# Softmax attention: turning the maxima on VectorE and gathering them by way of DRAM, in place of transposes on TensorE

## The chip, the core and the metric

The kernel runs on one core of a Trainium2 chip. A core has TensorE (PE in the profile, with its weight loads as PEld), VectorE (DVE), ScalarE (ACT), GpSimd (POOL), and SyncE (SP), which here only issues DMAs. The metric is the device time of one execution in microseconds. Before the change it is 2184.47 us, the median of three runs from 2184.06 to 2188.18.

## The reference

The input x has 2 sequences of 2048 tokens with 256 features each. The program is a chain of four residual blocks, each on a layer-normalized x: softmax attention (16 query heads in 4 groups over 4 key heads, head size 16), a feed-forward block of three rotation cycles, a linear causal attention, and the feed-forward block again. The change lies in the first of them:

```
q = x @ Wq + bq;  k = x @ Wk + bk;  v = x @ Wv + bv
scores = einsum('bghnd,bhsd->bghns', q, k)
attn   = softmax(scores / 4, axis=-1)
out    = einsum('bghns,bhsd->bghnd', attn, v)
return out.transpose(...).reshape(B, N, 256) @ Wo + bo
```

Everything is float32. The softmax subtracts each query's largest score before it takes the exponential.

## The kernel before

The attention is worked in 32 **units**. A unit is one block of 512 queries (8 blocks over the two sequences) in one of the 4 groups, with all 4 key heads r. Each unit is passed over twice.

The **first pass**, the generator `largest()`, finds the maxima. It has 64 steps per unit: for each of 4 key blocks of 512, 4 blocks of 128 queries (qi) and 4 heads (r), PE multiplies 128 queries by 512 keys into a PSUM tile `s` (L378, three banks, tag "s"), and VectorE reduces it to its maximum in a column of `mx` (L382). Behind the 64th step VectorE reduces `mx` to the negative maxima `nm` (L390) and splits each into two parts, a rounded one (L392) and the rest (L393). Both lie in `mt`, with queries on the partitions.

The **second pass** needs these numbers as rows, with the 512 queries along the free dimension. `turn_maxima` (L395) does that: four PE transposes into one PSUM bank `pm` (L398), a ScalarE copy of its 8 rows to `mr` (L402), and four small DMAs (L405) into `mrows`, two sets of two tiles that alternate from unit to unit. The row tiles are `a_m` in the profile.

In the second pass, for each unit and each of 16 key blocks of 128 (kb), PE computes transposed scores `p`, keys by queries, for four heads (L633). It adds the negative maxima by a second matmul into the same bank, `pick` times the rows of `mrows` (L637, the shift), ScalarE takes the exponential (L641), and PE multiplies the result by the values one iteration later (`weigh`, L620, eight matmuls in the trace). The four banks of `p`, with tag "p", are also where `pm` and other small results are put.

One iteration over kb therefore calls for four steps of the first pass (`next(ahead)`) and one of the second. The first pass runs 80 steps ahead. Its 64 steps for unit u+1 are done as kb 12 of unit u begins. Then `turn_maxima` is put in the list `later`; it is taken up at the beginning of kb 13, run behind that iteration's exponentials and ahead of its `weigh`. The rows are first read by the shifts in kb 0 of unit u+1. For unit 0 all of it falls into the prologue, where it runs at n == 67.

Other work around it: `finish` (L449) takes the sum of a unit in the kb loop of the next, over DMAs to DRAM and back (`ds`, `rs`, `dr`, `sums`, L465 to L475), and for every fourth unit multiplies by the output weights (L487) in four successive iterations, kb 10 to 13. `norm` (L414) prepares the next stage's input with PE transposes (L425). `project(u + 2)` stores a unit's queries to DRAM (L244) and loads them in the layout that both passes use (L249, `qP`, three buffers). Near the beginning of the loop the weights of the later stages are loaded (L686).

The order of instructions on each engine is written out by hand for the prologue (`in_order`, the SP queue among them) and again for the later stages. In the attention loop a scheduler puts the instructions of each engine in order by the program's order and by when it reckons them ready, so a transfer that is ready can go ahead of one that is not.

Of the kernel before, what the change touches and what calls it, by code (L numbers as in the profile page):

```python
# [9 lines left out]
F32 = mybir.dt.float32  # L10
F32R = mybir.dt.float32r
AF = mybir.ActivationFunctionType
ALU = mybir.AluOpType
AX = mybir.AxisListType
PSUM = bass.MemoryType.PSUM

P = 128
B, N, D = 2, 2048, 256
T = B * N
BLK = 512  # L20
# [4 lines left out]
KV = 4  # L25
# [42 lines left out]
def tile_hybrid(ctx: ExitStack, tc: tile.TileContext, x: bass.AP, consts: bass.AP, wa_d: bass.AP, wf_d: bass.AP, wb_d: bass.AP, out: bass.AP):  # L68
    nc = tc.nc
# [11 lines left out]
    dram = ctx.enter_context(tc.tile_pool(name="a_dram", bufs=2, space=bass.MemoryType.DRAM))  # L81
# [3 lines left out]
    def const(name):  # L85
        return small[:, _CONST[name][0] : _CONST[name][1]]
# [4 lines left out]
    ident, mean_w, ones = const("ident"), const("mean"), const("ones")  # L91
# [44 lines left out]
    def in_order(first, which=(engines.PE, engines.DVE, engines.Activation, engines.Pool)):  # L136

        last = {}
        for ins in nc.cur_bb.bb.instructions[first:]:
            if ins.engine in which:  # L140
                if ins.engine in last:
                    tc.add_manual_dep(
                        ins, last[ins.engine].name,
                        mybir.DependencyInfo(mybir.DependencyClass.NoSync, mybir.DependencyReason.DATA),
                        reason="order of the program",
                    )
                last[ins.engine] = ins
# [5 lines left out]
    def attention_a():  # L153
        with ExitStack() as st:
# [8 lines left out]
            mrows = [[hold.tile([P, BLK], F32R, name=f"a_m{i}_{p}") for p in range(2)] for i in range(2)]  # L163
# [10 lines left out]
            sb = st.enter_context(tc.tile_pool(name="a_sb", bufs=2))  # L174
            pss = st.enter_context(tc.tile_pool(name="a_s", bufs=3, space=PSUM))
            psp = st.enter_context(tc.tile_pool(name="a_p", bufs=4, space=PSUM))
# [182 lines left out]
                queries[u] = qP  # L359
                return lambda: fetch(qP, d)  # L360

            later = []

            def largest():


                for u, (j, g) in enumerate(units):
                    k0 = (j // BPB) * N
                    qP = queries[u]
                    mx = sb.tile([P, 4, KV, 4], F32, tag="mx", name=f"mx{u}")  # L370
                    first = u == 0

                    def step(kb, qi, r):

                        pool, tag = (psp, "p") if first and (4 * qi + r) % 5 > 2 else (pss, "s")
                        s = pool.tile([P, BLK], F32, tag=tag, name=f"s{u}_{kb}_{qi}_{r}")
                        row = slice(64 * (r % 2), 64 * (r % 2) + 64)
                        mm(  # L378
                            s, qP[r // 2][row, qi * P : (qi + 1) * P],
                            kP[r // 2][row, k0 + kb * BLK : k0 + (kb + 1) * BLK], start=True, stop=True,  # L380
                        )
                        nc.vector.tensor_reduce(mx[:, qi, r : r + 1, kb], s, AX.X, ALU.max)  # L382

                    for kb in range(4):
                        for qi in range(4):
                            for r in (0, 1, 3, 2):
                                step(kb, qi, r)
                                yield
                    nm = sb.tile([P, 4, KV], F32, tag="nm", name=f"nm{u}")
                    nc.vector.tensor_reduce(nm, mx, AX.X, ALU.max, negate=True)  # L390
                    mt = sb.tile([P, 4, KV, 2], F32, tag="mt", name=f"mt{u}")
                    nc.vector.tensor_copy(mt[:, :, :, 0].bitcast(F32R), nm)  # L392
                    nc.vector.tensor_tensor(mt[:, :, :, 1], nm, mt[:, :, :, 0], ALU.subtract)  # L393

                    def turn_maxima(u=u, mt=mt):  # L395
                        pm = psp.tile([P, BLK], F32, tag="p", name=f"pm{u}")
                        for qi in range(4):
                            nc.tensor.transpose(  # L398
                                pm[0 : 2 * KV, qi * P : (qi + 1) * P], mt[:, qi, :, :].rearrange("p r h -> p (r h)"), ident
                            )  # L400
                        mr = sb.tile([2 * KV, BLK], F32, tag="mr", name=f"mr{u}", bufs=1)
                        nc.scalar.copy(mr, pm[0 : 2 * KV, :])  # L402
                        for p in range(2):
                            for i in range(2):
                                nc.sync.dma_start(  # L405
                                    mrows[u % 2][p][64 * i : 64 * i + 2, :].bitcast(F32),
                                    mr[4 * p + 2 * i : 4 * p + 2 * i + 2, :],
                                )

                    later.append(turn_maxima)  # L410

            outs = {}

# [76 lines left out]

            LEAD, WARM = 64 + 16, 4
            ahead = largest()
            begin = len(nc.cur_bb.bb.instructions)
            loads = ExitStack()
# [111 lines left out]
            for n in range(4, LEAD):  # L606
                next(ahead)
                if n % 3 == 1:
                    next(rest, None)
                if n == 67:  # L610
                    for f in later:
                        f()
                    later.clear()
            in_order(begin, (engines.PE, engines.DVE, engines.Activation, engines.Pool, engines.SP))

            av, last, done, norms = None, None, iter(()), iter(())
# [8 lines left out]
            for u, kb in ((u, kb) for u in range(len(units)) for kb in range(KB)):  # L625
                qP, mrow = queries[u], mrows[u % 2]
                k0 = units[u][0] // BPB * N + kb * P
                t, es = [], []

                def score(r):  # L630
                    row = slice(64 * (r % 2), 64 * (r % 2) + 64)
                    t.append(psp.tile([P, BLK], F32, tag="p", name=f"p{u}_{kb}_{r}"))
                    mm(t[r], kP[r // 2][row, k0 : k0 + P], qP[r // 2][row, :], start=True, stop=False)  # L633

                def shift(r):
                    row = slice(64 * (r % 2), 64 * (r % 2) + 64)
                    mm(t[r], pick[row, :], mrow[r // 2][row, :], start=False, stop=True)  # L637

                def exp(r):
                    es.append(sb.tile([P, BLK], F32, tag="e", name=f"e{u}_{kb}_{r}", bufs=8))  # L640
                    nc.scalar.activation(es[r], t[r], AF.Exp, scale=1.0 / HD**0.5)  # L641

                ready = list(later)
                later.clear()

                next(ahead, None)
                next(ahead, None)
                score(0)
                score(1)
                shift(0)  # L650
                shift(1)
                exp(0)
                exp(1)
                if kb == 1:
                    next(done, None)
                score(2)
                next(ahead, None)
                score(3)
                shift(2)
                next(ahead, None)  # L660
                shift(3)
                exp(2)
                exp(3)
                for f in ready:
                    f()
                if last is not None:
                    if last[1] == 0:
                        av = pav.tile([P, BLK], F32, tag="av", name=f"av{last[0]}")
                    weigh(*last)
                    if last[1] == KB - 1:  # L670
                        done = finish(last[0], av)
                last = u, kb, es
                if kb > 1:
                    next(done, None)
                    next(norms, None)
                if u % G == 1 and kb == 1 and G < u < 4 * G:
                    norms = norm(u // G - 1)
                if kb == 4 and u + 2 < len(units):
                    project(u + 2)()
                if rest is not None and next(rest, "end") == "end":  # L680
                    rest = None
                    loads.close()
                    late = later_pools["late"] = ctx.enter_context(tc.tile_pool(name="late", bufs=1, side="right"))
                    for n, (name, of) in enumerate((("wf", wf_d), ("wb", wb_d))):
                        weights[name] = late.tile([P, of.shape[1]], F32, name=name)
                        nc.sync.dma_start(weights[name], of)  # L686
                    for name in ("w4", "b3"):
                        at = slice(*_WF[name])
                        nc.sync.dma_start(weights["wf"][64:P, at], wf_d[0:64, at])
# [21 lines left out]
    def behind(tail):  # L711
# [662 lines left out]
        in_order(begin)  # L1374

    behind(attention_a())


# [115 lines left out]
```

## Time and profile before

| | |
|---|---|
| median of three runs | 2184.47 us |
| the profiled execution | 2182.7 us |
| its span | 2180.8 us |
| granted TensorE clock, mean | 0.993 |
| attention stage in the trace | about 105 to 1565 us |
| PE, DVE, ACT busy in that stage | 1448, 1276, 1098 us |
| L402 copies, 32 | 559 ns each |
| L405 DMAs, 128 | 562 to 723 ns on SP's queue each |

The busy time of matmuls is modelled, since matmuls overlap one another, and 64-row matmuls on the two halves of the array run side by side. So a PE that is busy nearly all the time can still give time back. In rows of the timeline the first number is the start in us from the beginning of the span, the second the length; a mark like "x4" means that four instructions are merged, and brackets at the end give the idle time before and what ended it. "SPq" is the queue on which SP issues DMAs; its rows show the time of the issue, not of the data. An issue waits, and holds up what stands behind it on the queue, until what it depends on is there.

### The profile page before, as it was taken

Reading aid. Unit: us, or ns where it says so; the run is one execution under the profiler, and the core shown is the slowest. Engines: PE = TensorE matmul, PEld = TensorE weight load, DVE = VectorE, ACT = ScalarE, POOL = GpSimd, SP = SyncE. Lnnn points to the kernel's source line nnn. Section 1 sums busy time; section 2 is a strip of 40 time slices with the busy share of each in tenths; the row PEclk is TensorE's granted clock in tenths of the full one; section 3 lists DMA queues with packets and bytes.
Section 4 is the critical chain, followed back from the end, with each engine's and each line's share of the span. In section 5 each row is a group of like instructions: output and inputs, shape, how many; then the busy total and the mean of one; then the engine's idle time right before and its main releaser. Section 6 shows DMA issues by size and latency. Waiting matters only on the chain.

```text
span 2180.8 us, 38972 instructions
## 1 busy us (share of the span) xinstructions
PE 2136.0 (98%) x14346; PEld 1028.5 (47%) x14346; DVE 1725.7 (79%) x3319; ACT 1434.0 (66%) x2780; POOL 348.6 (16%) x318
## 2 busy tenths in 40 slices
PE   8899999999999999999999999999999999999998
PEld 3344444444444444444444444444444567676434
DVE  6789998998999899899899899987144688886435
ACT  3367777777776777777677777777864445554442
POOL 3100000000001000000000000000145345541450
PEclk9999999999999999999999999999999999999999
DMA  6410110101101011010110101100100000000002
GB/s 184 135 58 14 41 36 16 46 12 45 36 16 45 10 48 36 16 39 17 48 35 17 36 19 48 36 16 7 51 1 1 1 1 2 1 2 1 1 0 78
DMA packets 53552, 68.21 MB, mean 31 GB/s; under 512 B 18800, under 2 KB 27888, under 8 KB 53104
## 3 DMA queue, kind: packets, MB, share of 16 engines
q1 hardware_dynamic: 52448, 64.26, 10.6%
q8 instruction: 113, 1.85, 0.3%
q10 hardware_dynamic: 720, 0.92, 0.1%
q14 instruction: 79, 0.65, 0.1%
q0 software_dynamic: 192, 0.52, 0.1%
HBM read 35.26 MB, written 25.69 MB: 28 GB/s over the span
## 4 chain that ended last, share of the span: by engine, by line
PE 86%; DVE 8%; DMA 2%; ACT 1%; SPq 1%; issue 1%; POOL 1%; DVEq 0%; ACTq 0%; POOLq 0%
PE av L620 21%; PE s L378 19%; PE p L633 10%; PE q1f L796 7%; PE p L637 7%; DVE mx L382 5%; PE q2f L806 4%; PE pe L1084 2%; PE po L487 2%; PE bpo L1110 1%; PE pv L954 1%; PE pw L954 1%; PE pq L945 1%; PE q3f L816 1%; PE pk L945 1%; DMA xs<-in_x 1%
## 5 line engine op out<-in xcount | busy, mean ns | idle before, releaser
L382 DVE TENSOR_REDUCE mx<-s 128x1 f32<-128x512 f32 x2048 | 1272.9, 683 | 118.1 <-PE s L378 116.4
L641 ACT ACTIVATE e<-p 128x512 f32<-128x512 f32 x2048 | 1060.7, 605 | 356.9 <-PE p L637 353.3
L378 PE MATMUL s<-a_kP,qP 64*128 64x512 f32 x2048 | 706.7, 470 | 19.5 <-DVE mx L382 17.4
L637 PE MATMUL p<-a_m,a_pick 64*128 64x512 f32 x2048 | 589.5, 416 | 0.0
L378 PEld LDWEIGHTS s<-a_kP,qP 64*128 64x128 f32 x2048 | 283.1, 184 | 578.9 <-DVE mx L382 549.8
L620 PE MATMUL av<-e,a_v 128*32 128x512 f32 x4096 | 550.2, 605 | 0.0
L633 PE MATMUL p<-qP,a_kP 64*128 64x512 f32 x2048 | 529.1, 394 | 2.3 <-ACT e L641 2.3
L633 PEld LDWEIGHTS p<-qP,a_kP 64*128 64x128 f32 x2048 | 286.4, 185 | 62.8 <-ACT e L641 26.9
L637 PEld LDWEIGHTS p<-a_m,a_pick 64*128 64x128 f32 x2048 | 283.9, 184 | 29.4
L481 POOL TENSOR_TENSOR oc<-oc,sums 128x512 f32<-128x512 f32 x16 | 20.8, 1299 | 1232.7 <-DMA sums<-dr 907.1
L796 PE MATMUL q1f<-zq,wf 128*128 128x512 f32 x384 | 175.5, 600 | 0.0
L620 PEld LDWEIGHTS av<-e,a_v 128*32 128x32 f32 x4096 | 81.4, 108 | 128.5 <-issue 119.8
L797 ACT ACTIVATE a1f<-q1f,wf 128x512 f32<-128x512 f32 x96 | 66.0, 688 | 99.6 <-PE q1f L796 96.2
L796 PEld LDWEIGHTS q1f<-zq,wf 128*128 128x128 f32 x384 | 70.6, 190 | 98.0 <-issue 86.3
L806 PE MATMUL q2f<-a1f,wf 128*128 128x512 f32 x192 | 89.6, 610 | 0.0
L1090 DVE TENSOR_TENSOR en<-pe,small 128x512 f32<-128x512 f32 x128 | 79.4, 683 | 12.7 <-PE pe L1084 12.6
L835 DVE TENSOR_SCALAR cf<-cf,f_beta,alphaf 128x512 f32<-128x512 f32 x32 | 33.6, 1050 | 53.7 <-ACT cf L834 53.6
L839 POOL TENSOR_TENSOR tf<-cf,zq 128x512 f32<-128x512 f32 x32 | 55.6, 1737 | 92.0 <-DVE cf L835 91.7
L808 ACT ACTIVATE a2f<-q2f,wf 128x512 f32<-128x512 f32 x48 | 32.7, 687 | 54.9 <-PE q2f L806 54.9
L841 POOL TENSOR_TENSOR zq<-zq,tf 128x512 f32<-128x512 f32 x32 | 56.8, 1775 | 3.1 <-DVE tf L838 0.7
L806 PEld LDWEIGHTS q2f<-a1f,wf 128*128 128x128 f32 x192 | 35.2, 193 | 45.3 <-issue 44.4
L840 DVE TENSOR_TENSOR zq<-zq,tf 128x512 f32<-128x512 f32 x32 | 22.2, 693 | 36.2 <-POOL tf L839 36.0
(207 smaller groups left out, 1674.0 us busy)
## 6 DMA issues: line engine op xcount, KB each, us to landing
qP<-dq SPq DMA_DIRECT2D x64, 256.0 KB
dq<-qh SPq DMA_DIRECT2D x62, 128.0 KB
dq<-ql SPq DMA_DIRECT2D x62, 128.0 KB
a_kP<-dk SPq DMA_DIRECT2D x16, 256.0 KB
oc<-avs SPq DMA_DIRECT2D x128, 32.0 KB
sums<-dr SPq DMA_DIRECT2D x128, 32.0 KB
out<-xs SPq DMA_DIRECT2D x16, 256.0 KB
xs<-in_x SPq DMA_DIRECT2D x7, 512.0 KB
```

Source lines behind the costliest of these rows:

```text
L378: mm(s, qP[r // 2][row, qi * P : (qi + 1) * P], kP[r // 2][row, k0 + kb * BLK : k0 + (kb + 1) * BLK], start=True, stop=True,)
L382: nc.vector.tensor_reduce(mx[:, qi, r : r + 1, kb], s, AX.X, ALU.max)
L620: mm(av[32 * r : 32 * r + 32, :], vA[:, units[u][0] // BPB * KB + kb, 32 * r : 32 * r + 32], es[r], start=(kb == 0), stop=(kb == KB - 1),)
L633: mm(t[r], kP[r // 2][row, k0 : k0 + P], qP[r // 2][row, :], start=True, stop=False)
L637: mm(t[r], pick[row, :], mrow[r // 2][row, :], start=False, stop=True)
L641: nc.scalar.activation(es[r], t[r], AF.Exp, scale=1.0 / HD**0.5)
L796: mm(q1, w1[:, c, m * P : (m + 1) * P], z[:, c, :], start=(c == 0), stop=(c == 1))
L797: nc.scalar.activation(a1[:, m, :], q1, AF.Gelu, bias=b1[:, m : m + 1])
L806: mm(q2, w2[:, c, :], a1[:, c, :], start=(c == 0), stop=(c == 1))
L839: nc.gpsimd.tensor_tensor(t1, cs, z[:, 0, :], ALU.mult)
L841: nc.gpsimd.tensor_tensor(z[:, 1, :], z[:, 1, :], t1, ALU.subtract)
L1090: nc.vector.tensor_tensor(self.ens[t][w], pes[w].rearrange("p (h n) -> p h n", h=4), const("triu").unsqueeze(1).to_broadcast([P, 4, P]), A ...
```

## The change

The layouts of `mx`, `nm` and `mt` change, so that in `mt` the 32 columns stand as head, part, query block (r, i, q). Behind L393 VectorE transposes the 128x32 tile in squares of 32: in each group of 32 partitions b, row (r, i, q) of the result `mr` holds the values of 32 queries. Four DMAs, one for each group of partitions, write them to a DRAM tile `dm` of 8 rows by 512, in runs of 32 numbers (128 bytes). Four more load two rows each from there into `mrows`, and wait for the four stores. The PE transposes, the PSUM bank `pm`, the ScalarE copy, the function `turn_maxima` and the list `later` are gone. The whole sequence is now issued where the maxima are complete, in kb 12 (for unit 0 at n == 64), not an iteration later.

```diff
-                    mx = sb.tile([P, 4, KV, 4], F32, tag="mx", name=f"mx{u}")
+                    mx = sb.tile([P, KV, 4, 4], F32, tag="mx", name=f"mx{u}")
...
-                        nc.vector.tensor_reduce(mx[:, qi, r : r + 1, kb], s, AX.X, ALU.max)
+                        nc.vector.tensor_reduce(mx[:, r, qi : qi + 1, kb], s, AX.X, ALU.max)
...
-                    nm = sb.tile([P, 4, KV], F32, tag="nm", name=f"nm{u}")
+                    nm = sb.tile([P, KV, 4], F32, tag="nm", name=f"nm{u}")
                     nc.vector.tensor_reduce(nm, mx, AX.X, ALU.max, negate=True)
-                    mt = sb.tile([P, 4, KV, 2], F32, tag="mt", name=f"mt{u}")
-                    nc.vector.tensor_copy(mt[:, :, :, 0].bitcast(F32R), nm)
-                    nc.vector.tensor_tensor(mt[:, :, :, 1], nm, mt[:, :, :, 0], ALU.subtract)
-
-                    def turn_maxima(u=u, mt=mt):
-                        pm = psp.tile([P, BLK], F32, tag="p", name=f"pm{u}")
-                        for qi in range(4):
-                            nc.tensor.transpose(
-                                pm[0 : 2 * KV, qi * P : (qi + 1) * P], mt[:, qi, :, :].rearrange("p r h -> p (r h)"), ident
+
+                    mt = sb.tile([P, KV, 2, 4], F32, tag="mt", name=f"mt{u}")
+                    nc.vector.tensor_copy(mt[:, :, 0, :].bitcast(F32R), nm)
+                    nc.vector.tensor_tensor(mt[:, :, 1, :], nm, mt[:, :, 0, :], ALU.subtract)
+
+                    mr = sb.tile([P, 32], F32, tag="mr", name=f"mr{u}")
+                    nc.vector.transpose(mr, mt.rearrange("p r i q -> p (r i q)"))
+                    d = dram.tile([2 * KV, BLK], F32, tag="dm", name=f"dm{u}")
+                    for i in range(4):
+                        nc.sync.dma_start(
+                            d.rearrange("r (q b x) -> (r q) b x", b=4, x=32)[:, i, :], mr[32 * i : 32 * i + 32, :]
+                        )
+                    for p in range(2):
+                        for i in range(2):
+                            nc.sync.dma_start(
+                                mrows[u % 2][p][64 * i : 64 * i + 2, :].bitcast(F32),
+                                d[4 * p + 2 * i : 4 * p + 2 * i + 2, :],
                             )
-                        mr = sb.tile([2 * KV, BLK], F32, tag="mr", name=f"mr{u}", bufs=1)
-                        nc.scalar.copy(mr, pm[0 : 2 * KV, :])
-                        for p in range(2):
-                            for i in range(2):
-                                nc.sync.dma_start(
-                                    mrows[u % 2][p][64 * i : 64 * i + 2, :].bitcast(F32),
-                                    mr[4 * p + 2 * i : 4 * p + 2 * i + 2, :],
-                                )
-
-                    later.append(turn_maxima)
...
-                if n == 67:
-                    for f in later:
-                        f()
-                    later.clear()
...
-                ready = list(later)
-                later.clear()
...
-                for f in ready:
-                    f()
```

More of the change, by code (lines that the diff above doesn't have):

```diff
@@ L360, in project @@
                 return lambda: fetch(qP, d)
-            later = []
             def largest():
```

## The prediction

> **What bounds the kernel now.** I read first the page's table of busy time and its 40 slices, then the list of costliest groups, then the timeline of one unit of the attention stage, and last the timeline of SP's DMA queue over two units. The page's lines, and the rows that the change removes or sits beside:
>
> ```profile
> PE 2136.0 (98%) x14346; PEld 1028.5 (47%) x14346; DVE 1725.7 (79%) x3319; ACT 1434.0 (66%) x2780; POOL 348.6 (16%) x318
> ...
> L382 DVE TENSOR_REDUCE mx<-s 128x1 f32<-128x512 f32 x2048 | 1272.9, 683 | 118.1 <-PE s L378 116.4
> ...
> L398 PE MATMUL pm<-small,mt 128*8 128x128 f32 x128 | 19.2, 273 | 0.0
> L402 ACT COPY mr<-pm 8x512 f32<-8x512 f32 x32 | 17.9, 560 | 0.0
> ```
>
> The attention stage runs from about 105 to 1565 us. There PE is busy nearly all the time, and VectorE, which takes a maximum of every score block (L382), idles only 116 us in all for want of score blocks. The two are locked together: PE issues in order, and each score matmul (L378) waits for one of three PSUM banks that a maximum has to free. So a stretch of either engine can cost time, and busy shares can't tell which. I therefore cut the timeline of PE at the first L620 matmul of every iteration (one iteration is one key block, kb) and sorted the intervals by what else they hold. With nothing else in them 387 intervals have a median of 2.70 us. The two special kinds that matter stand one behind the other here (start, length, what):
>
> ```profile
> 788.14 0.50 PE L378 MATMUL s<-a_kP,qP 64*128 64x512 f32 x2
> ...
> 788.49 0.22 DVE L390 TENSOR_REDUCE nm<-mx 128x16 f32<-128x64 f32 x1
> ...
> 788.74 0.18 DVE L392 CAST mt<-nm 128x16 fp32r<-128x16 f32 x1
> ...
> 788.95 0.18 DVE L393 TENSOR_TENSOR mt<-nm,mt 128x16 f32<-128x16 f32 x1
> ...
> 789.04 2.48 DVE L382 TENSOR_REDUCE mx<-s 128x1 f32<-128x512 f32 x4
> ...
> 791.21 0.50 PE L378 MATMUL s<-a_kP,qP 64*128 64x512 f32 x2
> ...
> 792.92 0.60 PE L398 MATMUL pm<-small,mt 128*8 128x128 f32 x4
> ...
> 794.44 0.50 PE L378 MATMUL s<-a_kP,qP 64*128 64x512 f32 x2
> ...
> 794.78 2.64 SPq L405 DMA_DIRECT2D a_m<-mr  x4
> ...
> 797.15 0.50 PE L378 MATMUL s<-a_kP,qP 64*128 64x512 f32 x2
> ```
>
> Iterations begin at 788.14, 791.21, 794.44 and 797.15. The first (kb 12) holds VectorE's last steps on the maxima and takes 3.07; the second (kb 13) holds the four transposes and takes 3.23; the third takes the plain 2.71.
>
> **The parts of the change.** *Removed: the four transposes on PE and the bank they need.* Of 31 iterations with L398, 22 have a median of 3.24 against 2.70; seven that also hold the output projection (L487) take 4.30 against 3.76; two with the transposes of the next stage (L425) take 3.82 against 3.29. The price is the same 0.54 us each time, since PE stalls on nothing else there: 31 x 0.54 = **16.7 us gained**. VectorE can take the gain, for in those iterations it idles 0.7 us ahead of its maxima where it otherwise idles 0.2. Here a rule gives another size: "VectorE: DVE Perf Modes", section on the three transpose paths, puts a 128x128 transpose on TensorE at 390 ns (bf16). Four would be 1.56 us a unit and the gain 48 us. The row has 273 ns for one and 0.60 us for four overlapped; I take the row.
>
> *Removed: ScalarE's copy*, 32 x 560 ns = 17.9 us. ScalarE idles 357 us in all on L641's input, and in iterations with the copy PE's next p matmul starts 0.34 us after the iteration's beginning, as in the others. Worth nothing.
>
> *Added on VectorE: one transpose of 128x32 per unit*, right behind L393. The trace has none. The nearest rows are the cast of 128x16 (0.18 us) and the reduction of 128x64 (0.22); from start to start a step that needs the one before it takes its length and about 0.03 more. The same page section gives 311 ns for 128 columns of bf16; that is my upper end for 32 columns. I take 0.20 + 0.03 = 0.23, ends 0.10 (an instruction that overlaps its successor) and 0.34. Does it lie on the path? In the kb 12 shown, L390 to L393 push back the maxima by the 0.37 that the iteration is longer, so VectorE's slack of 0.2 is used up and more goes straight to the end. That holds in 21 iterations; in the nine where L390 shares its iteration with L487 or L425 the length doesn't change for it (3.76 and 3.29 with and without), so PE's extra work covers it, and unit 0's lies before the loop. 21 x 0.23 = **4.8 us lost** (2.1 to 7.1). Without the cover of the nine it would be 2.1 more. The changed layouts of mx, nm and mt keep sizes and instruction counts: nothing.
>
> *Moved and added on SP's queue: four DMAs become eight in two steps*, mr to DRAM (runs of 128 bytes), then DRAM to the rows. They start earlier, behind the VectorE transpose in kb 12, not behind ScalarE's copy in kb 13. What they must meet is the first shift matmul (L637) of the next unit, in the trace at 800.41, 11.46 us after L393 began; with 0.54 gone and 0.23 added it stands at +11.2. The rows for the two steps are those of another round trip through DRAM in each unit:
>
> ```profile
> 761.55 0.53 SPq L467 DMA_DIRECT2D rs<-ds  x1
> ...
> 763.58 0.34 SPq L473 DMA_DIRECT2D dr<-rs  x1
> 765.02 1.71 SPq L475 DMA_DIRECT2D sums<-dr  x4
> ```
>
> L475 waits for L473's data, so a store of 64-byte runs is usable 1.44 us after its issue; VectorE's reciprocal, which waits for L467, starts at 763.30, so a load takes 1.75. From L393's start: the transpose ends at +0.45; four stores at 0.59 (the queue's time for L244's) are issued by +2.9, the last begun at +2.3 and landed at +3.8; four loads at 0.66 (L405's) are begun by +5.8 and landed at **+7.6. 3.6 us are to spare**. Here a rule speaks against the change: "DMA: Bandwidth & Descriptors", Specifications, has transfers under 512 bytes read, modify and write[...]. The row for 64-byte runs already includes whatever it costs: 1.44. [...] So I put this at nothing, and if the cover were gone every microsecond of lateness would cost 31 us, since PE issues in order and stops at L637.
>
> The waits are new on SP's queue: the loads stand behind the stores' landing for some 1.5 us. Behind them comes only qP<-dq of the unit three ahead (L249, 15 units), which starts at about +9.0 when PE frees its buffer; by then the loads are issued. The stores of dq, avs and dr lie 10 us or more away on either side.
>
> *Unit 0* is different, for SP is kept in the order of the program there: the new stores stand behind a_kP<-dk, which ends at 100.87, 3.4 us after L393. Stores landed at +6.7 (first two loads issued then), their data at +9.3 to +9.6, against a first shift at 105.58, +8.1, in the trace. **About 1.5 us lost, once**; between nothing, if score blocks ahead fill the gap, and 8 us (below).
>
> *Sum:* -16.7 + 4.8 + 1.5 = -10.4. The profiled execution took 2182.7 (span 2180.8 and 1.9 around it), so 2172.3. The median of the runs shown lies 1.8 above that execution, and I give the forecast on its scale: **2174**.
>
> **The rivals.** *B, weights first.* Right behind L405 the trace issues the next stages' weights (L686, 0.73 and 1.20 MB) at 104.9. If they slip into the queue between unit 0's stores and loads, the loads queue behind them. The first landed 4.0 us after issue; less 1.75 that is 320 GB/s, so both take 6 us and unit 0's rows come some 7.7 us late, not 1.5. For it: the queue's order already puts ready transfers ahead of waiting ones (three oc<-avs ahead of rs<-ds, against the program). Against it: L686's own wait ended only about then. Then -4.2, 2180.
>
> *C, a costly transpose on VectorE.* The blocks of 32 might be slow. At 0.79 us, 21 of them eat up the 16.7. Against it: the rows of 0.18 to 0.25 and the 311 ns. At 0.7 the sum is near zero, 2184.
>
> *D, the rows come late: slower.* If the order on SP's queue puts qP<-dq ahead of the loads, they can't be issued before PE frees that buffer: L249 from +9.0 to +10.0, the first two loads by +10.6, landed 1.75 later behind 0.5 MB that takes up to 1.6 at the rate above (I take 0.6): +13.0 against +11.2, 1.8 x 15 = 27 lost, in all +17, 2191. It decides once the loads are issued later than +9. For it: loads now wait, and the order prefers what is ready. Against it: they are ready 5 us before L249 is. A round trip of over 11 us without any reordering would do the same.
>
> *E, the change frees nothing,* because VectorE sets the pace by itself. The 0.54 in 31 of 31 iterations speaks against it; it falls in with C.
>
> **How the numbers follow.** The likeliest case (-10.4; its own range 2169 to 2179, from -15 with a cheap transpose and no loss in unit 0 to -5.5 with 0.34 and a few us there) gets 0.60, B 0.14, C and E 0.08, D 0.18. About 0.2% (4.4 us) is what a measurement of this kernel can tell from no change. The likeliest case and half of B are faster, 0.67; the other half of B and a part of C same, 0.13; D and the rest of C slower, 0.20. The range from 2168 holds all but D, to 2186.
>
> **What will show it.** No L398 and L402 rows; kb 13 iterations back at 2.70; kb 12 at 3.3; a transpose of 0.2 us on VectorE. The loads of the rows should be issued 4 us after L393, ahead of qP<-dq, and the first L637 of each unit should show no wait on them. ScalarE waiting for L637 for more than 3.8 us at a unit's start would prove the forecast wrong, by B if only near 105 us, by D if in every second unit.

## The result and the profile after

The changed kernel takes 2174.77 us, the median of five runs from 2170.61 to 2176.11, against 2184.47 (2183.82 to 2188.28) for the kernel before beside it. The ratio is 0.9946, with a 95% interval of 0.9931 to 0.9961: faster by 0.4 to 0.7%, or 8.5 to 15.1 us. The two medians lie 9.7 us apart; the ratio, which is formed from all runs, stands for 11.8. The forecast was 2174, 10.4 us below the kernel before.

The profiled execution has a span of 2171.5 us, 9.3 shorter than before. The last copy of a sum (`avs`) ends the attention stage; from its start to the end of the span it is 617.2 us in both traces. So the whole difference lies in the attention. First the page's lines for the engines and the maxima, then the rows that took the place of L398 and L402, from the view of the tile `mr` (number of instructions, shortest, median and longest in ns, first and last start):

```profile
PE 2120.0 (98%) x14218; PEld 1019.6 (47%) x14218; DVE 1730.8 (80%) x3351; ACT 1417.8 (65%) x2748; POOL 348.8 (16%) x318
...
L380 DVE TENSOR_REDUCE mx<-s 128x1 f32<-128x512 f32 x2048 | 1270.6, 681 | 104.1 <-PE s L376 102.5
```

```profile
L398 SPq DMA_DIRECT2D dm<-mr x128: 302/420/1299, 101.3 to 1508.8; - x128
L395 DVE STREAM_TRANSPOSE mr<-mt x32: 210/211/214, 98.0 to 1507.3; 128x32 f32<-128x32 f32 x32
```

PE does 128 matmuls fewer, VectorE 32 transposes more at 0.21 us, and its idle time ahead of the maxima falls from 116 to 102 us. The timeline of the same unit as in the prediction, cut to the steps of the maxima, the starts of four iterations, and SP's queue:

```profile
784.29 0.50 PE L376 MATMUL s<-a_kP,qP 64*128 64x512 f32 x2
784.64 0.22 DVE L388 TENSOR_REDUCE nm<-mx 128x16 f32<-128x64 f32 x1
...
785.11 0.17 DVE L392 TENSOR_TENSOR mt<-nm,mt 128x16 f32<-128x16 f32 x1
785.31 0.21 DVE L395 STREAM_TRANSPOSE mr<-mt 128x32 f32<-128x32 f32 x1
...
785.45 2.44 DVE L380 TENSOR_REDUCE mx<-s 128x1 f32<-128x512 f32 x4
785.55 1.71 SPq L398 DMA_DIRECT2D dm<-mr  x4
...
787.58 0.50 PE L376 MATMUL s<-a_kP,qP 64*128 64x512 f32 x2
...
788.32 1.16 SPq L403 DMA_DIRECT2D a_m<-dm  x4
...
789.28 1.06 PE L612 MATMUL av<-e,a_v 128*32 128x512 f32 x8
...
790.27 0.49 PE L376 MATMUL s<-a_kP,qP 64*128 64x512 f32 x2
...
792.98 0.50 PE L376 MATMUL s<-a_kP,qP 64*128 64x512 f32 x2
793.77 1.00 SPq L249 DMA_DIRECT2D qP<-dq  x2
...
796.25 0.39 PE L629 MATMUL p<-a_m,a_pick 64*128 64x512 f32 x2
```

kb 12 takes 3.29 us (787.58 - 784.29) where it took 3.07, and kb 13 takes 2.69 where it took 3.23. The loads of the rows (L403) go out 3.2 us behind L392, ahead of L249, and the first shift of the next unit (796.25) comes 11.1 us behind it and waits for nothing.

Cutting the whole loop into iterations as the prediction does, and comparing the sums over each kind (us):

| kind of iteration | before | after | difference |
|---|---|---|---|
| the 31 that held L398, and those in the same place after | 108.7 | 92.2 | -16.5 |
| the 31 with nm and mt | 99.5 | 104.5 | +5.0 |
| the 31 with the reciprocal of the sums (L472, after: L468) | 88.3 | 90.8 | +2.5 |
| the 15 with the cast qh (L232) | 45.0 | 46.2 | +1.2 |
| from L392 (before: L393) of unit 0 to the first avs; unit 1's 0.33, counted in the first two rows, added back to the second value | 61.43 | 59.46 | -1.97 |
| ahead of that | 97.47 | 97.83 | +0.36 |

They add up to -9.4, which is the whole difference within rounding. Rows three, four and five are not in the forecast, or not with this sign. The last row is chance: L392 (L393) of unit 0 comes between 94.3 and 102.6 us over all the profiles of this record.

### The profile page after: what moved, and what is told of

Same layout as the page of the kernel before. It is cut to its first block, busy times and chain, and to the rows that moved or that the text cites. A ratio compares the mean times of both kernels' runs of the same rounds, so it can differ in the third digit from the quotient of the medians.

```text
span 2171.5 us, 38896 instructions
## 1 busy us (share of the span) xinstructions
PE 2120.0 (98%) x14218; PEld 1019.6 (47%) x14218; DVE 1730.8 (80%) x3351; ACT 1417.8 (65%) x2748; POOL 348.8 (16%) x318
## 4 chain that ended last, share of the span: by engine, by line
PE 85%; DVE 9%; DMA 2%; ACT 2%; issue 1%; SPq 1%; POOL 1%; ACTq 0%; DVEq 0%; POOLq 0%
PE av L612 21%; PE s L376 19%; PE p L625 10%; PE q1f L784 8%; PE p L629 6%; DVE mx L380 6%; PE q2f L794 4%; PE pe L1072 2%; PE po L483 2%; PE bpo L1098 1%; PE pv L942 1%; PE pw L942 1%; PE pq L933 1%; PE q3f L804 1%; PE pk L933 1%
## 5 line engine op out<-in xcount | busy, mean ns | idle before, releaser
L477 POOL TENSOR_TENSOR oc<-oc,sums 128x512 f32<-128x512 f32 x16 | 20.9, 1304 | 1226.1 <-DMA sums<-dr 1078.2
```

## The experiments

**Is it PE's own time? Put the transposes back.** On top of the change:

```diff
+                    def turn_again(u=u, mt=mt):
+                        pm = psp.tile([P, BLK], F32, tag="p", name=f"pm{u}")
+                        for qi in range(4):
+                            nc.tensor.transpose(pm[0 : 2 * KV, qi * P : (qi + 1) * P],
+                                                mt[:, :, :, qi].rearrange("p r i -> p (r i)"), ident)
+                    if u > 0:
+                        later.append(turn_again)     # run in kb 13, as before the change
```

> The changed kernel with four PE transposes of the parts put back into kb 13 of every unit but the first, into a bank that nothing reads; no ScalarE copy. Theory (the change gains because PE no longer stands 0.54 us per unit in its own stream): 31 x 0.54 = 16.7 us slower than the changed kernel, about 2191, and kb 13 iterations back at 3.24. Rival (the gain is the earlier start of the rows, or the copy and the held bank): within 3 us of the changed kernel, 2175 to 2178.

Measured: 2190.22 us (14 runs), 1.0018 of the kernel before (1.0010 to 1.0026). From 0.9946 that is 0.0072, or 15.7 us, of the 16.7 expected. The two ratios come from different chips, each against the kernel before on its own chip. The timeline of kb 12, 13 and the beginning of the next has the old step again, 3.25 us from 796.08 to 799.33:

```profile
792.79 0.51 PE L378 MATMUL s<-a_kP,qP 64*128 64x512 f32 x2
...
796.08 0.51 PE L378 MATMUL s<-a_kP,qP 64*128 64x512 f32 x2
797.80 0.60 PE L414 MATMUL pm<-small,mt 128*8 128x128 f32 x4
798.33 1.06 PE L625 MATMUL av<-e,a_v 128*32 128x512 f32 x8
799.33 0.50 PE L378 MATMUL s<-a_kP,qP 64*128 64x512 f32 x2
```

In this kernel the transposes feed nothing, so the earlier rows don't explain the gain. They take a bank of `p` again, but PE doesn't wait for it: L414 starts 1.72 us behind the iteration's first matmul, where the plain iteration of the changed kernel, above, has `weigh` at 1.70 (789.28 - 787.58). Four PE instructions in PE's own stream cost 0.54 us a unit.

**And the copy?** The same, with `nc.scalar.copy(mc, pm[0 : 2 * KV, :])` behind the transposes.

> As the run before, and ScalarE copies 8 rows of the bank (its result is not used). Theory: the copy lies in ScalarE's idle time, so within 1.5 us of the run without the copy, about 2191. Rival (the copy, and the bank held until it ends, were part of the price): 5 us or more above it.

Measured: 2189.65 us (12 runs), 1.0014 (1.0005 to 1.0024), not slower than without the copy. Its kb 13 iterations have the same 3.24. The copy, with the bank held until it ends, was worth nothing.

**What does the VectorE transpose cost?** Done twice, the second into an unused tile:

```diff
                     nc.vector.transpose(mr, mt.rearrange("p r i q -> p (r i q)"))
+                    nc.vector.transpose(again, mt.rearrange("p r i q -> p (r i q)"))
```

> The changed kernel with the VectorE transpose done twice, the second result unused. Theory (one costs its 0.21 us where PE's other work does not cover it): 22 to 24 x 0.21, so 4.6 to 5.1 us slower than the changed kernel, about 2179.5, and kb 12 iterations at 3.49. Rival (VectorE has room in that iteration and the 3.28 comes from something else): no change, 2175.

Measured: 2178.92 us (8 runs), 0.9966 (0.9956 to 0.9977), so on the slower side of the changed kernel, by 0.0020 or 4.4 us, though the two intervals overlap. The time alone would about fit the theory. The trace is sharper, and it denies the size: kb 12 has a median of 3.38, not 3.49, and the 31 iterations take 107.5 us in place of 104.5, so 3.0 more. Its VectorE steps:

```profile
791.69 0.18 DVE L392 TENSOR_TENSOR mt<-nm,mt 128x16 f32<-128x16 f32 x1
791.90 0.21 DVE L395 STREAM_TRANSPOSE mr<-mt 128x32 f32<-128x32 f32 x1
792.03 0.17 DVE L397 STREAM_TRANSPOSE again<-mt 128x32 f32<-128x32 f32 x1
792.13 2.44 DVE L380 TENSOR_REDUCE mx<-s 128x1 f32<-128x512 f32 x4
```

The first starts 0.21 behind L392, whose result it needs. The second needs nothing new and starts 0.13 behind the first; the maxima follow 0.10 later. So the second costs 0.10 and the first 0.21, of which about half is the wait for mt. Both are on the path, since the iteration grows by as much.

**How well is the round trip hidden?** Copies from DRAM to DRAM between the stores and the loads, one after the other, in every unit but the first:

```diff
+                    for hop in range(4 if u > 0 else 0):
+                        d, of = dram.tile([2 * KV, BLK], F32, tag=f"hop{hop}", name=f"hop{u}_{hop}"), d
+                        nc.sync.dma_start(d, of)
```

> The changed kernel with four copies from DRAM to DRAM, one after the other, between the stores and the loads in every unit but the first. The loads stand at 3.2 to 4.1 us behind L392 in the trace and their data is wanted at 11.1. With about 1.8 us a copy the loads go out at 10.5 and land at 12.3 or later, and in every second unit the load of the queries goes ahead of them or waits behind them. Theory (the round trip is hidden with 5 us to spare and a late row stops PE): 1 to 3 us a unit, 30 to 90 us slower than the changed kernel, 2205 to 2265. Rival (PE's order has enough other work to cover a late row): under 10 us slower.

Measured: 2253.75 us (2 runs), 1.031 (1.029 to 1.033): 79 us above the changed kernel, 2.5 us a unit. A unit of it, with L392 at 776.00:

```profile
776.45 1.70 SPq L398 DMA_DIRECT2D dm<-mr  x4
...
779.16 0.49 SPq L403 DMA_DIRECT2D hop<-dm  x1
...
781.12 4.48 SPq L403 DMA_DIRECT2D hop<-hop  x3
...
786.98 1.12 SPq L406 DMA_DIRECT2D a_m<-hop  x4
...
789.26 0.50 PE L632 MATMUL p<-a_m,a_pick 64*128 64x512 f32 x1
```

and from the view of the tile `a_m`, among what PE sat idle for (us, times):

```profile
  DMA a_m<-hop: 38.0, 35
```

A copy takes 1.96 us (779.16 to 781.12), the loads go out at +11.0 and the shift starts at +13.3. Late rows do stop PE, so the rival is out. The 2.5 us is a mean of two kinds of unit. In 22 units the first shift comes at least 2.1 us later than in the changed kernel, in the other nine by 0 to 0.6 us, and those are the units where the changed kernel has it at 11.75 to 14.8 us anyway. In eight of the 22 the load of the queries (L249) went out ahead of the rows, the order of rival D, and the shift was late by 2.4 to 4.3; in the others it was late by 2.1 to 2.2, but for the last unit (5.1). The late shifts add up to 57 us; what makes up the rest of the 79 is open.

> The changed kernel with two copies from DRAM to DRAM between the stores and the loads in every unit but the first. In the run with four, a copy took 1.95 us and the loads went out at 11 to 12 us behind L392. With two they go out at about 7.2 and land at about 9.2, ahead of the 11.1 at which the first shift asks for them, and ahead of the load of the queries at 8.7. Theory (5 us to spare): within 2 us of the changed kernel, 2173 to 2177. Rival (less room than the trace suggests): 15 us or more slower, 2190.

With two copies: 2178.11 us (4 runs), 0.9958 (0.9943 to 0.9973), no difference from the changed kernel that this measurement shows; the median is 1 us above the range of the theory and far from the rival's. A run below whose edit moved nothing (the weights asked for later) is the nearest thing to the changed kernel on the same chip, and took 2177.93. In the trace of the two copies the loads go out 7.1 to 9.2 us behind L392 in the 31 units that have them, ahead of L249 wherever one follows, and the first shifts stay where they are. So the round trip can grow by 4 us and still be hidden, and by 8 it is not.

**The start.** In unit 0 the first of the two weight loads did slip in between the stores and the loads, as rival B had it, and ScalarE waited 7.1 us for the first shift. Yet the stretch to the first avs became shorter. First the trace of the kernel before (L393 at 97.47), then the changed kernel's (L392 at 97.83):

```profile
102.10 7.35 DVE L382 TENSOR_REDUCE mx<-s 128x1 f32<-128x512 f32 x12 [2.06 <-PE s L378]
...
103.44 2.29 PE L378 MATMUL s<-a_kP,qP 64*128 64x512 f32 x4
...
105.58 0.39 PE L637 MATMUL p<-a_m,a_pick 64*128 64x512 f32 x1
...
112.20 1.29 DVE L382 TENSOR_REDUCE mx<-s 128x1 f32<-128x512 f32 x2 [0.88 <-PE s L378]
```

```profile
101.33 1.76 SPq L398 DMA_DIRECT2D dm<-mr  x4
...
101.77 10.28 DVE L380 TENSOR_REDUCE mx<-s 128x1 f32<-128x512 f32 x17 [1.15 <-PE s L376]
...
103.11 6.17 PE L376 MATMUL s<-a_kP,qP 64*128 64x512 f32 x10
103.19 0.37 SPq L674 DMA_DIRECT2D wf<-in_wf  x1
...
104.40 1.15 SPq L403 DMA_DIRECT2D a_m<-dm  x4
...
108.49 0.79 PE L629 MATMUL p<-a_m,a_pick 64*128 64x512 f32 x1
109.08 0.28 PEld L376 LDWEIGHTS s<-a_kP,qP 64*128 64x128 f32 x1 [0.31 <-DVE mx L380]
109.35 0.60 ACT L633 ACTIVATE e<-p 128x512 f32<-128x512 f32 x1 [7.08 <-PE p L629]
```

Between L392 and the first shift PE starts 18 score matmuls for the next unit, the last ten in a row, where the kernel before starts 12, and VectorE takes 17 maxima without a pause, not 12. That is work that the loop needs anyway. By 40 us behind L392 (L393) VectorE has taken 57 maxima of the next units in the changed kernel, and 54 in the kernel before. Three runs on it:

> The changed kernel, but unit 0 alone is turned as before the change (PE transposes and ScalarE copy at n == 67, rows straight from the copy), so its rows come before the weights of the later stages are asked for. In the traces the stretch from L392 of unit 0 to the first copy of a sum (avs) takes 61.4 us before and 59.1 after. Theory (the late rows of unit 0 cost nothing, because the maxima run ahead in the meantime): the stretch is 59.1 to 61.5, time 2174 to 2177. Rival (the wait of 7.1 us at the start costs 2 to 3 us, as the prediction has it): the stretch falls to about 57, time 2172.

With unit 0 alone turned on PE the stretch is 62.7 us, longer than the 59.1 and longer than either theory allowed, and the time is 2178.37 (5 runs), 0.9963 (0.9950 to 0.9976). The rival, that the late rows cost 2 to 3 us, falls: without them the start is 3.6 us longer in the trace. (The time can't tell: the run below whose edit moved nothing took 2177.93 on the same chip.) The difference is more than one profile's chance. Unit 0 is turned on PE in three profiles, this one, the kernel before and the kernel before with the edit of the next section, and their stretches are 61.4 to 62.8 us; in the seven with the changed kernel's own start, and no work added that reaches into it, they are 58.5 to 59.1. VectorE's pauses for score blocks in about the first 18 us behind L392 are 2.05, 0.23, 2.30 and 0.88 us here, where the changed kernel has 1.15, 0.20, 0.47 and 1.23.

> The changed kernel with the weights of the later stages asked for four iterations later, so that they no longer stand between the stores and the loads of unit 0's rows. Theory (late rows cost nothing at the start): first shift about 2 us earlier than the 108.5 of the trace, the stretch from L392 of unit 0 to the first avs within 0.5 us of 59.1, time 2174 to 2176. Rival (the weights ahead of the loads cost time): stretch and time fall by about 2 us, to 57 and 2172.5.

This run tells nothing on its question: moved to kb 4 in the program, the weights stayed where they were on the queue, 5.4 us behind L392, ahead of the loads: the scheduler pulled them forward. 2177.93 us (4 runs), 0.9954 (0.9939 to 0.9969), stretch 59.0. So the order was forced:

```diff
-                        nc.sync.dma_start(weights[name], of)
+                        tc.add_manual_dep(nc.sync.dma_start(weights[name], of).ins, first_rows[-1].name, ...)
```

> The changed kernel with the load of the later stages' weights held behind the loads of unit 0's rows on SP's queue (in the run before this, moving it in the program alone did not move it on the queue). In the changed kernel's trace the first shift starts 10.7 us after L392 of unit 0, right behind the tenth of ten score matmuls that the scheduler put ahead of it and that VectorE's maxima pace. Theory (that order, not the rows' landing, sets the first shift): still 10.5 to 10.9, the stretch from L392 to the first avs within 0.5 us of 59.1, time as the changed kernel's, 0.9945 of the kernel before. Rival (the weights hold up the rows, and the rows the shift): the shift comes 2 us earlier, the stretch falls to 57, 0.9935.

Now the loads go out ahead of the weights, and the first shift still comes 10.66 us behind L392 (at 99.69), with a stretch of 58.9:

```profile
104.97 6.17 PE L378 MATMUL s<-a_kP,qP 64*128 64x512 f32 x10
...
106.42 1.13 SPq L405 DMA_DIRECT2D a_m<-dm  x4
...
107.65 0.36 SPq L679 DMA_DIRECT2D wf<-in_wf  x1
...
110.35 0.79 PE L633 MATMUL p<-a_m,a_pick 64*128 64x512 f32 x1
```

The theory holds: what sets the first shift is the order that the scheduler gave PE. The DMA packets in the traces say the same. The last packet of unit 0's rows ends 9.25 us behind L392 in the changed kernel and 8.7 here, both ahead of the shift at 10.66; so the weights delayed the rows by some 0.6 us. That this order of PE also makes the start shorter rests on the profiles just compared; no run changed the order alone.

The time, 2180.46 (5 runs), 0.9965 (0.9950 to 0.9979), is above what the theory named, with an interval that excludes both 0.9945 and the rival's 0.9935. Its profiled run took 2174.97 at a granted clock of 0.992, the other four 2178.74 to 2181.59 at 0.989 and 0.990. Why they are longer was not traced. A profile of such a run exists for the weights asked for later: 2180.82 at 0.989. Its L392 of unit 0 comes 4.7 us later than in the changed kernel's profile, with a granted clock of 0.90 in the first 100 us against 0.93, and its part behind the attention is 1.8 us longer. Between the first avs and the last the two differ by 1.1 us alone.

**What costs as much as the change gains: the reciprocal.** The scheduler puts the reciprocal of a unit's sums three iterations ahead of its place in the program, where it reckons its data to be there. In the trace it is not always there (the row's brackets: idle before, and what ended it):

```profile
207.30 0.25 DVE L468 RECIPROCAL rs<-rs 128x16 f32<-128x16 f32 x1 [1.58 <-DMA rs<-ds]
```

The edit holds it back, in the changed kernel and in the kernel before:

```diff
-                nc.vector.reciprocal(rs, rs)
+                tc.keep_in_program_order(nc.vector.reciprocal(rs, rs))
```

> The changed kernel with the reciprocal of the sums (L468) held at its place in the program, three iterations later than the scheduler puts it. In the trace of the changed kernel the 31 iterations with L468 take 90.8 us where 31 plain ones take 83.7, and VectorE waits there for the load of rs. Theory (that wait stops the maxima and so PE): these iterations fall to 2.71 each, 5 to 7 us faster than the changed kernel, about 2168.5. Rival (VectorE catches up by itself, or the wait moves elsewhere): within 1.5 us of the changed kernel.

> The kernel before, with the reciprocal of the sums (L472) held at its place in the program. In its profile the 31 iterations with L472 take 88.3 us against 83.7 for plain ones, and the 15 with the cast qh 44.9 against 40.6. Theory (the early reciprocal costs the kernel before about 9 us too, and the change's own worth is 0.33 us a unit and a start that is 2 us shorter, 12 us in all): about 2177, 12 us above the changed kernel with the same edit. Rival (the change made the reciprocal worse, or only shifted its waits): under 5 us gained here, and the distance between the two pinned kernels over 16 us.

> The changed kernel as it is, on the chip of the run before it, so that the three forms can be compared side by side. Theory: 0.9945 of the kernel before, and above the changed kernel with the pinned reciprocal by 11 us. Rival (the chip of the first comparison was favourable): 0.998 or more.

> The changed kernel with the pinned reciprocal, on the chip of the two runs before it. Theory: 0.989 of the kernel before, with a spread of the runs under 2 us, since the varying wait for rs is gone. Rival: a part of its lead was the chip's, 0.992 or more.

The first gave 2164.18 us (4 runs), 0.9893 (0.9877 to 0.9910). The other three ran on one chip beside the kernel before, which took 2188.97 there:

| | median us | runs | ratio to the kernel before, interval |
|---|---|---|---|
| kernel before, reciprocal held | 2176.52 | 2174.90 to 2178.24 | 0.9944 (0.9932 to 0.9957) |
| changed kernel | 2176.06 | 2175.42 to 2177.32 | 0.9944 (0.9931 to 0.9956) |
| changed kernel, reciprocal held | 2162.77 | 2159.99 to 2163.98 | 0.9878 (0.9863 to 0.9893) |

The two edits add up: the hold is worth 12.5 us before the change and 13.3 after it, and the change 12.9 us without it and 13.8 with it. The theory had 5 to 7 and "about 9" for the hold: right in kind, too small. The theory of a spread under 2 us, in the fourth of these texts, did not come true: the runs with the hold lie 4.0 us apart, those without it 1.9. So the waits for rs are not what spreads the times. They do differ between profiles: in one stretch of the stage (105 to 1500 us) VectorE waits for rs, in the view of the waits, 9.3 us in the first profile of the changed kernel,

```profile
DVE rs L468 <- DMA rs<-ds: 9.3, 14, 1.6
```

and 13.3 us in the second one, 22 times and up to 2.4 us. With the hold that row is gone, and the 31 iterations take 83.3 us, no more than plain ones. The 15 with qh fall from 46.2 to 40.8, which had not been expected to this extent: behind the early reciprocal GpSimd's product of the sums (L477) also comes early, and meets VectorE's cast. These are rows of the changed kernel, then of the one with the hold:

```profile
580.66 1.29 POOL L477 TENSOR_TENSOR oc<-oc,sums 128x512 f32<-128x512 f32 x1 [60.02 <-PE p L629]
...
581.62 0.61 DVE L232 CAST qh<-zq 128x512 fp32r<-128x512 f32 x1
```

```profile
577.52 0.42 DVE L232 CAST qh<-zq 128x512 fp32r<-128x512 f32 x1
...
590.71 1.29 POOL L477 TENSOR_TENSOR oc<-oc,sums 128x512 f32<-128x512 f32 x1 [11.40 <-DMA sums<-dr]
```

## Why the prediction was right

*PE's transposes (16.7 us gained).* Right: 16.5 in the trace, and 15.7 when they were put back. The price read from pairs of iterations with and without them (0.54 us) held in all three kinds. The busy time of L398, 19.2 us, would have been near by luck; the estimate of 48 us from the 390 ns in "VectorE: DVE Perf Modes" of the Trainium skill, section on the three transpose paths, was not.

*ScalarE's copy (nothing).* Right: with it and without it the time is the same.

*VectorE's transpose (4.8 us lost, ends 2.1 and 7.1).* Right: 0.21 us for one, 0.21 longer iterations, 5.0 us in the sum. The cover by PE's other work held for four of the seven iterations with the output projection. Three that also held statistics of the next stage went from 3.76 to 3.94, and the two with L425 kept their 3.29. The doubled transpose shows what the lower end meant: an independent one would have cost 0.10.

*The round trip (hidden, 3.6 us to spare).* Right, and too careful. Four stores took 1.71 us on the queue, not 2.4, and four loads 1.16, not 2.6: the rows of wider transfers were the wrong likeness for these. In the unit shown the last packet of the rows ends 5.2 us behind L392, 5.9 ahead of the shift. With two copies added it still was hidden, with four it cost 2.5 us a unit. The place of the first shift, +11.2, was met within 0.1 (11.15 in most units). The order on SP's queue, on which rival D hung, was as forecast in all 15 units that have both: L403 ahead of L249.

*Unit 0 (1.5 us lost).* **This step failed.** Its times were right: the stores landed and the loads went out 6.6 us behind L392 where it had 6.7, and the last packet of the rows ended at 9.25 where it had 9.3 to 9.6. But the start became about 2 us shorter, not 1.5 longer. The step took the first shift for the thing that must not be late. The runs show that the shift's place, 10.66, is set by the order that PE was given, and that PE and VectorE do the maxima in the meantime. It had named this case ("if score blocks ahead fill the gap") and not chosen it. Rival B's transfer happened in part: the first weights, 0.73 MB, went in between, and delayed the rows by 0.6 us, not by about 6. The sign that was to prove the forecast wrong, ScalarE waiting more than 3.8 us near 105 us, appeared (7.1 us at 109.35) and proved nothing of the kind: the runs show no cost of this wait.

*Rival D's number.* Its loss of 27 us makes the sum +17, so 2201 on the forecast's scale. The 2191 given is a slip.

*Left out.* The reciprocal's early place and the cast's collision with GpSimd cost the kernel before some 12 us, and in these two profiles 3.8 us more after the change. Whether the change made them worse can't be said: the waits differ as much between two profiles of the changed kernel, and with both kernels' reciprocals held the change is worth 13.8 us, against 12.9 without.

So the forecast of 10.4, for 9.4 in the two traces and 9.7 between the medians, is two right terms and two misses that nearly cancel, 3.5 us better at the start and 3.8 worse in the loop. That they cancel is luck: on another chip the change was worth 12.9.

## What to carry to other kernels

Where two engines are locked together by a few buffers, cut the timeline into iterations and compare those with and without an operation: the difference prices it, which neither busy time nor an instruction's length does. A longer chain of small DMAs in place of a step on the bounding engine costs nothing as long as its landing lies ahead of its reader by more than its own spread; measure that lead by adding hops. And look at where the scheduler puts work that waits for a DMA: holding one reciprocal of 0.25 us at its place was worth as much as this whole change.

## What the runs showed of the hardware

VectorE's cast of 128x512 from float32 to the rounded form, SBUF to SBUF, takes 0.41 us alone (all 15 of the kernel with the hold lie between 0.41 and 0.42) and up to 1.30 us in the changed kernel. "SBUF — State Buffer" of the Trainium skill, section on the two separate sides, has VectorE and GpSimd share a pair of ports, which the first to start keeps for its whole instruction. The traces agree, in both directions. In the changed kernel's, 12 of the 15 casts start while GpSimd's product L477 runs, and each of them ends 0.28 or 0.29 us behind the product's end, however early it started (581.62 + 0.61 against 580.66 + 1.29 in the rows above). In two the cast starts first, by 0.1 us: it takes its 0.41, and the product takes 1.45 and 1.47 in place of about 1.28. A copy of 16 KB from DRAM to DRAM took 1.96 us from issue to the next one's issue, and a store in runs of 128 bytes was not slow: the loads that wait for four of them went out 2.8 us behind the first store's issue.
